# Dealing VectorE's and ScalarE's work anew beside one head's second product in a graph attention kernel

## The chip, the cores and the metric

The kernel runs on one core of a Trainium2 chip. The metric is the device time of one execution in microseconds (us), the median of several runs. The profile comes from one further execution, taken by the hardware profiler. TensorE (PE) multiplies matrices, VectorE (DVE) and ScalarE (ACT) work elementwise, GpSimd (POOL) issues here almost only DMAs that add to what they find (accumulating DMAs), and SyncE (SP) issues plain and transposing DMAs.

## The reference

Two graph attention layers over 512 nodes of 768 features, with a residual and a layer norm. The first layer has 8 heads, whose outputs are concatenated (512 x 6144) and pass through an ELU; the second has one head. All in float32.

```python
def gat_layer(x, W, a_s, a_d, b, edge_index, concat):
    n = x.shape[0]
    H, C = a_s.shape
    h = (x @ W).reshape(n, H, C)
    src, dst = (edge_index[0], edge_index[1])
    alpha_s = jnp.einsum('nhc,hc->nh', h, a_s)
    alpha_d = jnp.einsum('nhc,hc->nh', h, a_d)
    e = jax.nn.leaky_relu(alpha_s[src] + alpha_d[dst], NEG_SLOPE)
    m = jax.ops.segment_max(e, dst, num_segments=n)
    e = jnp.exp(e - m[dst])
    denom = jax.ops.segment_sum(e, dst, num_segments=n)
    alpha = e / (denom[dst] + EPS)
    msg = h[src] * alpha[:, :, None]
    out = jax.ops.segment_sum(msg, dst, num_segments=n)
    ...
h = gat_layer(x, W1, a_src1, a_dst1, b1, edge_list, concat=True)
h = jax.nn.elu(h)
out = gat_layer(h, W2, a_src2, a_dst2, b2, edge_list, concat=True)
...
x = _layernorm(x + out, axis=-1)
```

## The kernel before

The edges are counted once into a dense 512 x 512 table, so that attention becomes dense: for each head a matrix of 512 x 512 scores, a softmax along its rows, and a product with the head's features. The matrix lies in four tiles of 128 rows (tile 0 to 3). The order of all engines is written out by hand; each engine runs its own instructions strictly in that order and waits for others through semaphores.

A head goes through four stages. The first product makes its features (x times its 768 columns of W1). The scores of its attention are made beside other products. The aggregation multiplies features and attention and passes through the ELU to gT. The second product multiplies gT by the head's 768 rows of W2 and adds to h2, the input of the second layer. The first product and the second product run in a fast scheme with fewer multiplications: the operands are cut into thirds and sums of them are multiplied, 15 products named P0 to P14, in the order P13, P2, P8, P4, P12, P9, P6, P0, P1, P14, P10, P5, P11, P7, P3. This document numbers them 0 to 14 by that order and also speaks of them by name. Each has eight matmul instructions in the profile (L480).

The loop `for h in range(H - 1)` holds at h = 6 (`last`) the second product of the seventh head, with the scores of the eighth head beside it. For each product n of the loop, `multiply()` issues the matmuls, then the list `plan[n]` is issued, and `empty()` takes the result out of its PSUM bank into h2. The pieces:

- `empty()` is, by default, an addition on VectorE straight from PSUM (L493). For the pieces of h2 listed in `by_dma` it is a copy by ScalarE to a buffer in SBUF (L490) and an accumulating DMA from POOL (L491). In the seventh head only the piece (1, 2), which P13, P8 and P0 feed, goes by DMA; in the heads before also (0, 0), which P2 and P7 feed, and (0, 2). The 15 products belong to five chains, each with one PSUM bank: P13, P4, P6, P14, P7 share one, P2, P12, P0, P10, P11, P3 another, P1 and P5 a third, P8 and P9 have one each. A product can start when its chain's bank has been emptied.
- `sum_up(...)` issues on VectorE the sums of gT that a product reads (L1073, L1076); `of_b(...)` those of the weights (L170), of which only P3's is left for this stage; P7's is an accumulating DMA of POOL (L133) behind product 1.
- `score(t)` makes tile t of the scores on ScalarE (`lift`, L636). `scored(t)` is `leak` on VectorE (L640), `rank` on VectorE (L645, count and row maximum) and the exponential on ScalarE (L649), which also gives the row sums `den`.
- `weigh(q, t)` makes one over the row sum on VectorE (L878 and L879, `rden`) and, unless `scale=False`, multiplies the tile by it on VectorE (L881).
- The weighted tiles must be transposed into PT. Tiles 0 and 1 go by DMA: `turn_out` copies the tile (L898, ScalarE), SP issues a transposing DMA (L900), and `turn_in` copies the result into PT (L903, ScalarE). With `rden` given, `turn_out` first scales the tile on ScalarE (L895). Tiles 2 and 3 are turned by TensorE: `turn` is four transposes (L887) and a copy into PT by ScalarE (L888).

In the seventh head before, `weigh` with scaling follows products 7, 9, 11 and 13 for tiles 0 to 3; `turn_in` of tiles 0 and 1 follows products 12 and 13; `turn` of tile 2 stands ahead of product 14, that of tile 3 inside it, before its last two matmuls.

Behind product 14 `last_sum()` has POOL issue one accumulating DMA into w2r for the second layer (L118, 576 KB); SP loads x again (L99). Then the last aggregation (`aggregate`, L921) multiplies all of PT and the eighth head's features in six steps of 128 columns; beside it VectorE forms the second layer's logits from h2 (L424), and the second layer's products follow (L409, L1414).

Of the kernel before, what the change touches and what calls it, by code (L numbers as in the profile page):

```python
# [13 lines left out]
AF = mybir.ActivationFunctionType  # L14
# [23 lines left out]
def gat_pass(  # L38
# [16 lines left out]
    nc = tc.nc  # L55
    P = 128
    N, D = x.shape
    H = a_src1.shape[0]
# [373 lines left out]
    def by_halves(hs, XA, B_):  # L432
# [4 lines left out]
        def pair(p, i, start, empty):  # L437
            def multiply():
                if start:
# [17 lines left out]
                 P1=("z", (0, 1), -1.0), P10=("y", (1, 1), -1.0), P5=("z", (1, 1), 1.0), P14=("x", (0, 1), -1.0),  # L457
                 P11=("y", (0, 1), 1.0), P7=("x", (0, 0), -1.0), P3=("y", (0, 2), -1.0))
# [44 lines left out]

    def second_by_thirds(h, A_, B_):
        return by_thirds(h2, A_, B_, ("P13", "P2", "P8", "P4", "P12", "P9", "P6", "P0", "P1", "P14", "P10", "P5", "P11", "P7", "P3"),
                         False, ((1, 2), (0, 0), (0, 2)) if h + 2 < H else ((1, 2),))

    def second(A_, B_):

# [168 lines left out]
    if not general:  # L678
# [95 lines left out]
        for n, batch in enumerate(batches):  # L774
# [10 lines left out]
            while n < len(wants) and pos < wants[n]:  # L785
# [3 lines left out]
                multiply, empty, on_vector = items[pos]  # L789
# [17 lines left out]
            if n + 1 == len(batches):  # L807
                spread(0)
                q = [lift(0, t) for t in range(NT)]
# [11 lines left out]
    else:  # L821
# [26 lines left out]
        q = [lift(0, t) for t in range(NT)]  # L848
# [20 lines left out]
    def weigh(q, t, scale=True):  # L869

        if folded:
            den = dens.pop(t)
        else:
            den = small.tile([P, 1], F32, name="den")
            nc.vector.scalar_tensor_tensor(q, q, 1.0, cnt[:, t, :], op0=ALU.mult, op1=ALU.mult,
                                           accum_out=den)
        rden = small.tile([P, 1], F32, name="rden")
        nc.vector.tensor_scalar(rden, den, EPS_DEN, None, op0=ALU.add)  # L878
        nc.vector.reciprocal(rden, rden)  # L879
        if scale:  # L880
            nc.vector.tensor_scalar(q, q, rden, None, op0=ALU.mult)  # L881
        return rden

    def turn(q, t):
        ps = tr.tile([P, 512], F32, name="tr")
        for s in range(NT):
            nc.tensor.transpose(ps[:, s * P:(s + 1) * P], q[:, s * P:(s + 1) * P], ident)  # L887
        nc.scalar.copy(PT[:, :, t * P:(t + 1) * P], ps[:, :N].rearrange("p (s d) -> p s d", d=P))  # L888
# [4 lines left out]
    def turn_out(q, t, rden=None):  # L893
        if rden is not None:
            nc.scalar.activation(q, q, AF.Copy, scale=rden)  # L895
        apart = pS[:, t].rearrange("p k n -> p (k n)") if t < 3 else work.tile([P, N], F32, name="nr")
        apart = apart.bitcast(U16)
        nc.scalar.copy(apart.rearrange("p (h n) -> p h n", h=2), q.bitcast(U16).rearrange("p (n h) -> p h n", h=2))  # L898
        parted[t] = work.tile([P, N], F32, name="zr", bufs=3).bitcast(U16)
        nc.sync.dma_start(parted[t].rearrange("p (j d) -> p j d", d=P), apart, transpose=True)  # L900

    def turn_in(t):
        nc.scalar.copy(PT.rearrange("p s n -> p (s n)").bitcast(U16).rearrange("p (s n h) -> p s n h", s=NT, h=2)[  # L903
            :, :, t * P:(t + 1) * P, :], parted.pop(t).rearrange("p (h s d) -> p s d h", h=2, s=NT))
# [206 lines left out]
    def out_by_dma(t):  # L1111
        turn_out(q[t], t, weigh(q[t], t, scale=False))

    for h in range(H - 1):
        last = h + 2 == H
        q = {}
# [12 lines left out]
        if h == 0:  # L1129
            GA, gsums = left(gT, gS)  # L1130
            finish = mixed(0, AA, BB, [[besides[:1], [besides[1], sources[0]]], [[sources[1]], [sources[2]] + row],
                                       [besides[2:], list(targets)]])
            load_w1(2)()
            load_a(2, a_src1[2], a_dst1[2])
            attend = attended(0)
            pairs = by_halves(h2, GA, B2)
            for m, _ in pairs[:2]:
                m()
            pairs[0][1]()
            for f in finish:  # L1140
                f()
            gsums[0]()
            pairs[1][1]()
            gsums[1]()
            pending[0]()
            pairs[2][0]()
            gsums[2]()
            pairs[3][0]()
            gsums[3]()
            pending[1]()  # L1150
            pairs[2][1]()
            pairs[3][1]()
            fold_count(0)
            score(0)
            for n in range(2, 7):
                (m0, e0), (m1, e1) = pairs[2 * n:2 * n + 2]
                m0()
                m1()
                if n < 6:
                    scored(n - 2)  # L1160
                if n < 5:
                    score(n - 1)
                if n == 6:
                    turn_in(0)
                    out_by_dma(2)
                e0()
                if 3 < n < 6:
                    out_by_dma(n - 4)
                if n == 6:
                    out_by_dma(3)  # L1170
                    B2, sums2, load_pairs, load_first, load_rest = load_second(1)
                    load_pairs()
                    load_first()
                    load_rest()
                e1()
                if n < 5:
                    fold_count(n - 1)
        else:
            G, gsums = g_thirds(h)

            def of_b(*names):
                return [sums2.pop(p) for p in names if p in sums2]

            amid = [[], of_b("P6", "P2"), behind] if h == 1 else [of_b("P1"), [], of_b("P4")]
            finish = mixed(h, AA, BB, [[[sources[0]], [sources[1]] + amid[0]], [row, [targets[0]] + amid[1]], [amid[2], [targets[1]]]],
                           [gsums[p] for p in ("P13", "P8")])
            behind = []
            if not last:
                load_a(h + 2, a_src1[h + 2], a_dst1[h + 2])
                attend = attended(h)  # L1190
            pairs = second_by_thirds(h, G, B2)

            def sum_up(*names):
                return [gsums[p] for p in names]

            def at(f, *args):
                return [lambda: f(*args)]

            plan = {0: of_b("P6") + sum_up("P14") + finish[:1], 1: finish[1:] + of_b("P4") + sum_up("P12"), 2: sum_up("P9", "P7"),
                    3: sum_up("P1") + at(score, 0), 4: sum_up("P6"), 5: at(scored, 0) + at(score, 1), 6: of_b("P1") + sum_up("P10"),  # L1200
                    7: at(scored, 1) + at(score, 2), 8: sum_up("P5") + of_b("P3"), 9: at(scored, 2) + at(score, 3),
                    10: sum_up("P11"), 11: at(scored, 3), 12: [], 13: sum_up("P3")}
            if h > 1:
                plan[0][1:1] = [plan[13].pop()]
            behind_it = {1: of_b("P7")}

            def also(n, *what):
                plan[n] = plan.get(n, []) + list(what)

            for n, f in zip((8, 10), in_second):  # L1210
                also(n, f)
            if not last:
                for f in attend:
                    also(13, f)
            for n, (multiply, empty) in enumerate(pairs):
                if last and n == 14:
                    turn(q[2], 2)
                    multiply(lambda: turn(q[3], 3))
                else:
                    multiply()  # L1220
                for f in plan.get(n, []):
                    f()
                if last and n in (7, 9, 11):
                    weigh(q[(n - 7) // 2], (n - 7) // 2)
                    if n < 11:
                        turn_out(q[(n - 7) // 2], (n - 7) // 2)
                if last and n > 11:
                    if n < 14:
                        turn_in(n - 12)
                    if n == 13:  # L1230
                        weigh(q[3], 3)
                empty()
                if not last and n == 13:
                    turn_in(0)
                for f in behind_it.get(n, []):
                    f()
                if last:
                    continue
                if n in (7, 9, 11, 14):
                    out_by_dma(min(n - 7, 6) // 2)  # L1240
                if n == 5:
                    B2, sums2, load_pairs, load_first, load_rest = load_second(h + 1)
                    load_pairs()
                if n == 14:
                    rest_of_thirds()
                    reload_x()
                    load_first()
                    load_rest()
# [68 lines left out]
    finish = []  # L1317
# [150 lines left out]
```

## Time and profile before

| | |
|---|---|
| median of 3 runs | 639.59 us (639.29 to 639.63) |
| the profiled execution | 639.91 us, of which the span from the first to the last instruction is 638.0 us |
| second product of the seventh head, first product to the last aggregation's start | 526.22 to 556.53 us |
| last aggregation (L921) | 556.53 us to 579.09 us |
| mean granted TensorE clock | 0.995 |

The span is the time from the first instruction's start to the last one's end; times in the text are counted from its start. A timeline row gives an instruction's start, its duration, engine, line, operation, output and inputs and how many were merged; in square brackets stands the engine's idle time ahead of it and what ended that. Ends of matmuls are modelled by the profiler. Weight loads (PEld) run beside matmuls.

### The profile page before, as it was taken

Reading aid. Unit: us, or ns where it says so; the run is one execution under the profiler, and the core shown is the slowest. Engines: PE = TensorE matmul, PEld = TensorE weight load, DVE = VectorE, ACT = ScalarE, POOL = GpSimd, SP = SyncE. Lnnn points to the kernel's source line nnn. Section 1 sums busy time; section 2 is a strip of 40 time slices with the busy share of each in tenths; the row PEclk is TensorE's granted clock in tenths of the full one; section 3 lists DMA queues with packets and bytes.
Section 4 is the critical chain, followed back from the end, with each engine's and each line's share of the span. In section 5 each row is a group of like instructions: output and inputs, shape, how many; then the busy total and the mean of one; then the engine's idle time right before and its main releaser. Section 6 shows DMA issues by size and latency. Waiting matters only on the chain.

```text
span 638.0 us, 8411 instructions
## 1 busy us (share of the span) xinstructions
PE 623.7 (98%) x2725; PEld 477.2 (75%) x2725; DVE 523.3 (82%) x1112; ACT 329.8 (52%) x579; POOL 146.2 (23%) x174
## 2 busy tenths in 40 slices
PE   8999999999999999999999999999999999899995
PEld 5555586556888888888888888888888888645553
DVE  8979989788898878968896879878897879656775
ACT  4875775640658146741757055832756164443440
POOL 1300011023342332313352332413432302100000
PEclk9999999999999999999999999999999999999999
DMA  8993397789999998999899998999899983810122
GB/s 294 328 239 91 69 257 256 175 221 254 251 214 166 297 261 201 183 294 234 200 209 228 265 247 209 166 330 240 174 206 263 238 260 50 160 52 1 33 58 78
DMA packets 108207, 126.82 MB, mean 199 GB/s; under 512 B 41542, under 2 KB 89342, under 8 KB 107390
## 3 DMA queue, kind: packets, MB, share of 16 engines
q1 hardware_dynamic: 74718, 90.17, 45.3%
q0 software_dynamic: 33008, 35.46, 36.2%
q10 hardware_dynamic: 432, 0.59, 0.3%
q8 instruction: 23, 0.38, 0.2%
q14 instruction: 26, 0.21, 0.1%
HBM read 98.66 MB, written 2.90 MB: 159 GB/s over the span
## 4 chain that ended last, share of the span: by engine, by line
PE 87%; DVE 6%; DMA 3%; ACT 2%; issue 1%; SPq 0%; DVEq 0%; ACTq 0%
PE mm L480 40%; PE mm L974 18%; PE mm L409 16%; PE mm L921 4%; PE mm L1414 3%; PE held L409 2%; PE tr L742 1%; DMA zr<-pS 1%; DMA w2r<-in_L_gnn_W_dram 1%; DMA w2t<-in_L_gnn_a_dst_dram 1%; DVE h L493 1%; DVE q L645 1%; DVE q L640 1%; PE bc L276 1%; PE held L608 1%
## 5 line engine op out<-in xcount | busy, mean ns | idle before, releaser
L486 ACT ACTIVATE hs<-mm 128x512 f32<-128x512 f32 x30 | 17.9, 596 | 88.9 <-PE mm L480 70.8
L974 PE MATMUL mm<-PT,hs 128*128 128x256 f32 x252 | 61.3, 379 | 0.0
L649 ACT ACTIVATE q<-q,nmax 128x512 f32<-128x512 f32 x32 | 23.1, 722 | 60.2 <-DVE nmax L645 60.2
L493 DVE TENSOR_TENSOR hs<-hs,mm 128x512 f32<-128x512 f32 x45 | 30.8, 684 | 27.7 <-PE mm L480 26.1
L974 PEld LDWEIGHTS mm<-PT,hs 128*128 128x128 f32 x252 | 47.8, 190 | 7.2 <-ACT u L978 0.3
L491 POOL DMA_DIRECT2D h<-pass x22 | 26.5, 1313 | 89.2 <-ACT pass L490 79.3
L493 DVE TENSOR_TENSOR h<-h,mm 128x512 f32<-128x512 f32 x57 | 38.9, 684 | 7.3 <-PE mm L480 6.8
L974 PE MATMUL mm<-pS,gS 128*128 128x256 f32 x168 | 43.1, 379 | 0.0
L903 ACT COPY PT<-zr 128x1024 uint16<-128x1024 uint16 x34 | 39.2, 1154 | 5.8 <-DMA zr<-pS 5.2
L480 PE MATMUL mm<-w2r,gT 128*128 128x256 f32 x160 | 37.9, 385 | 0.0
L480 PE MATMUL mm<-w2r,xT 128*128 128x256 f32 x160 | 37.8, 379 | 0.0
L133 POOL DMA_DIRECT2D w1t<-in_L_gnn_W_dram x18 | 29.4, 1651 | 29.6 <-PE mm L409 26.8
L974 PEld LDWEIGHTS mm<-pS,gS 128*128 128x128 f32 x168 | 31.9, 190 | 4.3
L480 PE MATMUL mm<-w1t,hs 128*128 128x256 f32 x144 | 34.3, 381 | 0.5 <-DVE h L493 0.5
L480 PEld LDWEIGHTS mm<-w2r,gT 128*128 128x128 f32 x160 | 29.6, 190 | 6.6 <-DVE hs L493 3.0
L480 PE MATMUL mm<-w1r,hs 128*128 128x256 f32 x144 | 34.2, 379 | 0.0
L480 PE MATMUL mm<-w1r,gS 128*128 128x256 f32 x144 | 34.0, 379 | 0.0
L480 PEld LDWEIGHTS mm<-w2r,xT 128*128 128x128 f32 x160 | 30.4, 190 | 4.1
L978 ACT COPY u<-mm 128x256 f32<-128x256 f32 x21 | 7.8, 371 | 45.7 <-PE mm L974 45.7
L480 PEld LDWEIGHTS mm<-w1t,hs 128*128 128x128 f32 x144 | 27.1, 190 | 5.1 <-DVE h L493 1.3
L716 DVE TENSOR_SCALAR os<-nodes,idx 128x512 bf16<-128x512 f16 x104 | 29.1, 352 | 1.4 <-PE tr L742 1.4
L480 PEld LDWEIGHTS mm<-w1r,gS 128*128 128x128 f32 x144 | 27.4, 190 | 3.7
(281 smaller groups left out, 1543.4 us busy)
## 6 DMA issues: line engine op xcount, KB each, us to landing
w2r<-in_L_gnn_W_dram SPq DMA_DIRECT2D x48, 384.0 KB
w1r<-in_L_gnn_W_dram SPq DMA_DIRECT2D x43, 384.0 KB
gT<-xd SPq DMA_DIRECT2D x5, 1280.0 KB
w1t<-in_L_gnn_W_dram SPq DMA_DIRECT2D x24, 256.0 KB
h<-pass POOLq DMA_DIRECT2D x22, 256.0 KB, 3.9
w1t<-in_L_gnn_W_dram POOLq DMA_DIRECT2D x18, 256.0 KB, 5.8
w2t<-in_L_gnn_W_dram SPq DMA_DIRECT2D x15, 256.0 KB
w2t<-in_L_gnn_W_dram POOLq DMA_DIRECT2D x15, 256.0 KB, 9.1
```

Source lines behind the costliest of these rows:

```text
L133: nc.gpsimd.dma_start(o, i, accum_op=ALU.add)
L409: nc.tensor.matmul(ps[:, :HALF], A_[p][:, k, i * P:(i + 1) * P], B_[p][:, k, :], start=start and k == 0, stop=k == HK - 1, skip_group_chec ...
L480: nc.tensor.matmul(bank[chain][:, i * TH:(i + 1) * TH], A_[p][:, k, i * P:(i + 1) * P], B_[p][:, k, :], start=first and i == k == 0, stop= ...
L486: nc.scalar.activation(out(o), ps, AF.Copy, scale=sign)
L491: nc.gpsimd.dma_start(out(o), part, accum_op=ALU.add)
L493: nc.vector.tensor_tensor(out(o), out(o), ps, op=ALU.add if sign > 0 else ALU.subtract)
L649: nc.scalar.activation(q, q, AF.Exp, bias=nmax, scale=-1.0, accum_out=dens[t])
L716: nc.vector.tensor_scalar(o, nodes, idx[:, c:c + 1], None, op0=ALU.is_equal)
L903: nc.scalar.copy(PT.rearrange("p s n -> p (s n)").bitcast(U16).rearrange("p (s n h) -> p s n h", s=NT, h=2)[:, :, t * P:(t + 1) * P, :], p ...
L921: nc.tensor.matmul(ps[:, :N], HS[h][:, s, c * P:(c + 1) * P], PT[:, s, :], start=(s == 0), stop=(s == NT - 1))
L974: nc.tensor.matmul(bank[p][:, :HN], A_[p][:, k, c * P:(c + 1) * P], B_[p][:, k, :], start=over is None and k == 0, stop=k == 1, skip_group ...
L1414: nc.tensor.matmul(ps[:, :cols.stop - cols.start], PT[:, s, t * P:(t + 1) * P], h2[:, s, cols], start=(s == 2), stop=(s == 1))
```

## The change

In the seventh head's second product alone:

- The piece (0, 0) of h2, fed by P2 and P7, is emptied by a ScalarE copy and an accumulating DMA instead of VectorE.
- The plan is written anew for this head: the sums of P14 and P3 go from product 0 to products 5 and 11, the other sums, too, partly change places, the scores start behind product 1 instead of 3, tile by tile one to two products earlier, and P3's weight sum goes from product 8 to 12.
- All four tiles are scaled by ScalarE: tiles 0 and 1 in `turn_out` behind products 7 and 9, tiles 2 and 3 by a new helper `scale` behind products 11 and 12.
- Tile 2 is turned ahead of product 13 and tile 3 ahead of product 14. Both `turn_in` follow product 13, behind tile 2's turn and ahead of tile 3's in ScalarE's order.
- As POOL works in order, its DMA for P7 now stands ahead of L118 of `last_sum()`.

```diff
     def second_by_thirds(h, A_, B_):
         return by_thirds(h2, A_, B_, ("P13", "P2", "P8", "P4", "P12", "P9", "P6", "P0", "P1", "P14", "P10", "P5", "P11", "P7", "P3"),
-                         False, ((1, 2), (0, 0), (0, 2)) if h + 2 < H else ((1, 2),))
+                         False, ((1, 2), (0, 0), (0, 2)) if h + 2 < H else ((1, 2), (0, 0)))
...
+    def scale(t):
+        nc.scalar.activation(q[t], q[t], AF.Copy, scale=weigh(q[t], t, scale=False))
+
...
+            third_sum = of_b("P3")
             plan = {0: of_b("P6") + sum_up("P14") + finish[:1], 1: finish[1:] + of_b("P4") + sum_up("P12"), 2: sum_up("P9", "P7"),
                     3: sum_up("P1") + at(score, 0), 4: sum_up("P6"), 5: at(scored, 0) + at(score, 1), 6: of_b("P1") + sum_up("P10"),
-                    7: at(scored, 1) + at(score, 2), 8: sum_up("P5") + of_b("P3"), 9: at(scored, 2) + at(score, 3),
+                    7: at(scored, 1) + at(score, 2), 8: sum_up("P5") + third_sum, 9: at(scored, 2) + at(score, 3),
                     10: sum_up("P11"), 11: at(scored, 3), 12: [], 13: sum_up("P3")}
             if h > 1:
                 plan[0][1:1] = [plan[13].pop()]
+            if last:
+                plan = {0: finish[:1], 1: finish[1:] + sum_up("P12") + at(score, 0), 2: sum_up("P9", "P7"), 3: sum_up("P1"),
+                        4: sum_up("P6") + at(scored, 0) + at(score, 1), 5: sum_up("P14"), 6: sum_up("P10") + at(scored, 1) + at(score, 2),
+                        7: at(out_by_dma, 0) + sum_up("P5"), 8: sum_up("P11") + at(scored, 2) + at(score, 3), 9: at(out_by_dma, 1),
+                        10: at(scored, 3), 11: at(scale, 2) + sum_up("P3"), 12: third_sum + at(scale, 3), 13: at(turn_in, 0) + at(turn_in, 1)}
...
             for n, (multiply, empty) in enumerate(pairs):
-                if last and n == 14:
-                    turn(q[2], 2)
-                    multiply(lambda: turn(q[3], 3))
-                else:
-                    multiply()
+                if last and n > 12:
+                    turn(q[n - 11], n - 11)
+                multiply()
                 for f in plan.get(n, []):
                     f()
-                if last and n in (7, 9, 11):
-                    weigh(q[(n - 7) // 2], (n - 7) // 2)
-                    if n < 11:
-                        turn_out(q[(n - 7) // 2], (n - 7) // 2)
-                if last and n > 11:
-                    if n < 14:
-                        turn_in(n - 12)
-                    if n == 13:
-                        weigh(q[3], 3)
                 empty()
```

## The prediction

> **What bounds the kernel now.** I read the page first: one core, TensorE busy nearly throughout, so a change beside it can only win back time in which TensorE stands still or runs slowly.
>
> ```profile
> span 638.0 us, 8411 instructions
> PE 623.7 (98%) x2725; PEld 477.2 (75%) x2725; DVE 523.3 (82%) x1112; ACT 329.8 (52%) x579; POOL 146.2 (23%) x174
> ```
>
> Then the timeline of TensorE around the seventh head's second product. Its fifteen products start at 526.22. The last two matmuls of product 14 start at 553.11, and the last aggregation (L921) starts after an idle 2.83 us, the largest hole between matmuls in the run.
>
> ```profile
> 553.11 0.60 PE L480 MATMUL mm<-w1r,hs 128*128 128x256 f32 x2
> 556.53 22.56 PE L921 MATMUL mm<-PT,hs 128*128 128x512 f32 x48 [2.83 <-ACT PT L888]
> ```
>
> The chain of waits says what the aggregation waited for: tile 1's copy for the turning DMA (L898), that DMA, which took 7.34 us, ScalarE's copy-in (L903), and both copies of the TensorE-turned tiles 2 and 3 (L888), queued behind it.
>
> ```profile
> 546.02 0.94 ACT pS L898
> 546.97 0.02 issue
> 546.98 7.34 DMA zr<-pS
> 554.33 0.02 issue
> 554.35 1.16 ACT PT L903
> 555.51 0.98 ACT PT L888 x2
> 556.49 0.04 issue
> 556.53 22.56 PE mm L921 x48
> ```
>
> Why 7.34 us? The DMA view, over the 3.52 us after that issue and over tile 0's issue, one fence each: in the first stretch no packet of SP's queue q1 moves, and POOL's q0 has 96.1% of the engines.
>
> ```profile
> q0 software_dynamic: 363, 0.52, 96.1%
> ```
>
> ```profile
> q1 hardware_dynamic: 1056, 0.26, 42.4%
> ```
>
> The second line is tile 0's transfer: all its 1056 packets lie within 543.06 to 545.80, 2.74 us from the issue. q0 in the first stretch is L118, the 576 KB accumulation into w2r that POOL issued at 544.53, ahead of tile 1's transfer.
>
> Last, the windows of the granted clock (columns: stretch, length, busy time and instructions of PE, PEld, DVE, ACT, POOL, clock, DMA share, GB/s).
>
> ```profile
> 549.90:553.31 3.41, 3.41 (x21) 3.02 (x20) 2.04 (x6) 0.66 (x1) 0.00 (x0) 1.00 1.39 135
> 553.31:556.72 3.41, 0.58 (x3) 0.19 (x2) 0.76 (x2) 2.13 (x3) 0.00 (x0) 1.00 0.56 162
> 556.72:560.13 3.41, 3.41 (x5) 1.35 (x5) 0.00 (x0) 0.00 (x0) 0.00 (x0) 0.50 1.00 392
> 560.13:563.54 3.41, 3.41 (x10) 1.50 (x9) 0.00 (x0) 1.58 (x3) 0.00 (x0) 1.00 0.07 29
> 628.40:631.81 3.41, 2.56 (x16) 2.18 (x14) 2.78 (x8) 0.00 (x0) 0.00 (x0) 1.00 0.31 120
> ```
>
> After a stretch with TensorE busy for 0.58 of 3.41 us, the next 3.41 us run at clock 0.50: five matmuls where the next stretch has ten. The hole costs twice: 2.83 us empty, and a slow start. From the aggregation's start to the next product (578.93) are 22.40 us; its 48 matmuls at the 0.429 us pitch of the later ones would take 20.59. The slow start is 1.81 us. All that can be had here is 2.83 + 1.81, and small stalls in front of products 10 and 12 (0.45 us: product 13 starts 22.99 us after product 0, where 1.83 and twelve times 1.726 make 22.54): some 5 us.
>
> **The change, part by part.** Prices are start to start, from rows of this stretch and of the sixth head's, which already scales on ScalarE.
>
> VectorE loses the emptying of P2 and P7 (L493, 0.60 each) and four scalings (L881, 0.40, 0.60, 0.40, 0.40): 3.0 us. ScalarE gains two copies (L490, 0.49 each), two scalings in front of the DMA copy (L895 then L898 of the same tile, 0.74) and two in front of a turn (0.62 by the same row): 3.7 us. ScalarE is busy for 9.86 of the 19 us from 538 to 557, so there is room; where it is not free is the order, below.
>
> POOL gets two more accumulations (P2's and P7's, L491, 256 KB). P2's stands ahead of B's P7 sum (L133, 531.30 before), which moves back by about 1 us; that sum took 4.5 us and product 13 reads it at 549. P8's accumulation waits for P13's landing (534.2) as before. P7's stands ahead of L118: L118 moves from 544.53 to about 554, behind the copy of P7. Its reader is the last layer's P7 product, at 594.64 now and 589.8 then; the longest landing of that line is 17.1 us, so it is in by 571. Cost nothing.
>
> Now the order, replayed with the rows' prices. TensorE unstalled: 526.22, a first product of 1.83, fourteen at 1.726, two turns of 0.44: product 13 ends at 551.1, the turn of tile 3 at 551.4, product 14 at 553.25.
>
> VectorE: the sums of P14 and P3 no longer precede the finish, so L915 starts at 528.6 instead of 529.8. Then P12, P9, P7, P1 to 532.9; P4's emptying waits for product 3 (533.4). Leak 0 at 534.6 (535.76 before): tile 0's q was made at 530.2, behind P13's copy on ScalarE. That q needs the row broadcast, whose issue at 523.38 lies seven us earlier. From there each tile costs VectorE leak, rank, rden (0.72, 0.62, 0.27) and about three L493 or sums (0.60 each); leaks fall at 534.6, 538.4, 541.8 and 544.8, the last held for 0.2 us by tile 3's q on ScalarE. Rank 3 ends at 546.2. Then P10's emptying, rden 2 (547.1), P3's sum, P5's emptying, B's P3 sum, rden 3 (549.2), P11's emptying (549.8).
>
> ScalarE: scale 0 at 541.2, behind tile 2's q; copy 0 ends 542.9. Then P0's copy (ends 543.45; product 10 reads that bank at 543.5, a margin of nothing and a stall of at most 0.1, as before), exp 2, q 3, scale 1 at 544.7, copy 1 ends 546.46; exp 3 at 546.4, scale 2 at 547.1, and scale 3, which waits for rden 3, at 549.2 to 549.9. Behind scale 3 the queue holds L888 of tile 2 (549.8), L903 twice (550.3, 551.4), P7's copy (552.45) and L888 of tile 3 (552.9 to 553.5): with scale 3 six instructions, 4.3 us, all in front of the aggregation. P10's emptying ends 546.84; product 12 follows in that bank at 547.05. The turn of tile 2 needs scale 2 (547.9) at 548.8, that of tile 3 scale 3 (549.9) at 550.95: both in time.
>
> Turning DMAs: tile 0 issued 543.0, tile 1 546.5. L118 is gone from that stretch; what is left is P0's 256 KB accumulation, which before was issued 0.8 us after tile 0's and let it pass in 2.74 us. Bounds for tile 1: 2.74 (tile 0's row) and 7.34 us; I take 2.74, as the thing that stood in the way has gone: landed 549.2, wanted at 551.4.
>
> So the aggregation starts at the later of TensorE's 553.25 and ScalarE's 553.5 plus 0.06: 553.56 instead of 556.53, **2.97 us** earlier. TensorE is idle for 0.3 us, less than the 0.85 us not busy in the last window shown, which was followed by clock 1.00; so the slow start goes too, **1.81 us**. Sum 4.8 us. After that everything hangs on TensorE: the DVE view shows holes of 0.9, 0.6 and 2.0 us before 581, and nothing else moves.
>
> The halved clock also has a page in the Trainium skill: TensorE: Matmul & The Clock Gate, section "What's actually happening", gives at least one idle window of about 3.4 us as what halves the clock. The hole here is 2.83 us and TensorE worked for 0.58 us of the window, and yet the next one ran at 0.50: read strictly, the rule would leave the clock alone, and a change that only closes the hole would give 2.97 us; the trace speaks against it.
>
> The profiled run took 639.91 us (span 638.0 and 1.9 around it), 0.32 over the median of 639.59. 639.91 - 4.8 = 635.1, in terms of the median **634.8 us**.
>
> **The rivals.** (a) The scores don't come that fast. Between leaks the seventh head has 3.46, 3.92 and 4.11 us now, the sixth 3.40, 3.45 and 3.52, my replay 3.7, 3.4, 3.0. At 3.45 for the last, everything behind moves by 0.4 us (635.2). At 4.11 throughout, leak 3 falls at 547.0, 2.1 late; the hole is 2.4 us and the clock may halve again: 636.9 to 638.7. For: VectorE and ScalarE wait for one another four times. Against: the sixth head's rows, with the same scaling. Chance 0.11.
>
> (b) The slow start isn't the hole's doing. Then only 2.97 us come: 636.6. Against: the halved stretch follows the one nearly idle window before the end, and no other. By the Trainium skill's rule above this would be the outcome. Chance 0.04.
>
> (c) Tile 1's transfer is late for another reason, 7.34 us as now. It lands at 553.8; L903, P7's copy and L888 put the start at 556.0, the hole and the clock stay: 639.1, no change to speak of. Chance 0.04.
>
> (d) Slower: P7's accumulation. It is issued at 553.05, as SP starts the five loads of 384 KB that wait for product 14. The first logits of the last layer (L424) read those columns at 559.65, and VectorE stands in order behind them. L491's landings go from 3.6 to 10.4 us in this trace, the long ones beside such loads: 556.7 to 563.5. VectorE's holes before 581 take up 3.4 us, so up to a landing at 563 it is free, and at 10.4 us it costs 0.5. It eats the whole gain at 567.9 (559.65 + 3.4 + 4.8), 14.8 us after the issue, and past that the kernel is slower: at 17.1 us, the longest landing of a 576 KB accumulation, the last layer starts 7.1 us late and the time is 641.9. Chance 0.03; with what I don't see, slower gets 0.05.
>
> **How the numbers follow.** My forecast has 0.78: 634.8, and for itself 634.2 (start at TensorE's 553.25, nothing late on ScalarE) to 635.9. The range reaches into (a) and over (b): 634.0 to 637.0; left out are the late part of (a), (c) and (d). This kernel's three runs lie within 0.34 us, so about 0.2%, 1.3 us, can be told from no change. Faster by more than that (below 638.3): the forecast, (a) nearly whole, (b): 0.91. Same 0.04, slower 0.05.
>
> **What would show it.** In the profile after: no idle over 0.5 us in front of L921, and released by L888; the aggregation's 48 matmuls in 20.8 instead of 22.56 us, clock 1.00 there; tile 1's DMA off the chain; L118 issued after 553; ScalarE without a hole from scale 3 to L888. Wrong would be: a DMA still on the chain in front of L903, a hole on ScalarE in front of scale 3 with rden 3 after 550, or L424 waiting for the accumulation into h.

## The result and the profile after

The changed kernel takes 634.93 us (median of 6 runs, 634.20 to 635.21) against 639.61 us: a ratio of 0.993, 95% interval 0.9912 to 0.9947. The forecast was 634.8 us. The profiled execution took 634.52 us with a span of 632.7 us.

TensorE's timeline, the two rows that answer to those of before (start, duration, what, in brackets the idle time ahead and what ended it):

```profile
550.80 1.89 PE L480 MATMUL mm<-w1r,hs 128*128 128x256 f32 x8
552.97 20.87 PE L921 MATMUL mm<-PT,hs 128*128 128x512 f32 x48 [0.28 <-ACT PT L888]
```

The hole of 2.83 us is 0.28 us, and the aggregation's 48 matmuls take 20.87 instead of 22.56 us. The first product starts at 525.56 here, at 526.22 before: what lies ahead of the change differs from execution to execution (525.15 to 526.24 in the ten profiles of this case), so stretches are compared, not places. The whole of that difference is there before the first L409 matmul, which starts at 10.24 to 11.37 us; from it to product 0 all ten take 514.85 to 514.94 us. From product 0 to the aggregation's start it is 27.41 us (30.31 before, -2.90), from there to the next product 20.71 us (22.40, -1.69), and from there to the end 59.0 us in both. The two differences make 4.6 us.

The chain of waits in front of the aggregation no longer has a DMA in it:

```profile
548.38 0.17 DVE rden L879
...
548.64 0.72 ACT q L1115
549.36 0.47 ACT PT L888
549.83 0.33 ACT PT L903
550.16 0.63 issue
550.79 1.16 ACT PT L903
551.96 0.49 ACT pass L490
552.45 0.48 ACT PT L888
```

It is ScalarE's queue from tile 3's scaling on, without idle time (the 0.63 us of "issue" lie inside the first of two L903, which ScalarE's timeline shows as busy throughout).

The DMA view of the 3.52 us after the issue of tile 1's turning DMA (queue, packets, MB, share of 16 engines), the same stretch that before showed q0 alone:

```profile
q1 hardware_dynamic: 1053, 0.26, 36.4%
q0 software_dynamic: 101, 0.09, 16.5%
```

1053 of the transfer's 1056 packets are through; before, none was. And the windows of the clock around the start (stretch, length, busy times, then clock, DMA share, GB/s):

```profile
549.56:552.97 3.41, 3.13 (x17) 2.42 (x15) 0.24 (x1) 3.36 (x5) 0.22 (x1) 1.00 0.00 0
552.97:556.38 3.41, 3.41 (x8) 1.63 (x9) 0.52 (x2) 0.00 (x0) 2.27 (x2) 1.00 0.74 186
```

The clock stays at 1.00.

One thing about the time before must be known to read it. The 42 runs of the kernel before that stood beside the experiments fall into two groups: 15 had a mean clock of 0.997 or more and a median of 637.33 us (637.09 to 638.45), the other 27 had 0.991 to 0.996 and times from 638.78 us on, and the 19 of them at 0.995 or 0.996 a median of 639.82 us. The profiled execution, with its halved clock behind the hole, is one of the second group (0.995). So about two executions in three seem to be slowed behind the hole, and the median is of such a one. No execution of the first group was profiled. Nor is the hole's slow start all that parts the groups: they lie 2.5 us apart, and it costs 1.7 to 1.8. Part of the rest may be the start of an execution, where the profiles differ by up to 1.1 us; this was not tested. Against the first group the change is worth 637.33 - 634.93 = 2.4 us. The changed kernel's twelve times lie within 1.1 us.

### The profile page after: what moved, and what is told of

Same layout as the page of the kernel before. It is cut to its first block, busy times and chain, and to the rows that moved or that the text cites. A ratio compares the mean times of both kernels' runs of the same rounds, so it can differ in the third digit from the quotient of the medians.

```text
span 632.7 us, 8415 instructions
## 1 busy us (share of the span) xinstructions
PE 621.1 (98%) x2725; PEld 476.6 (75%) x2725; DVE 520.1 (82%) x1106; ACT 333.1 (53%) x585; POOL 148.6 (23%) x176
## 4 chain that ended last, share of the span: by engine, by line
PE 85%; DVE 7%; DMA 4%; ACT 2%; issue 1%; SPq 1%; DVEq 0%; POOLq 0%; ACTq 0%
PE mm L480 39%; PE mm L974 17%; PE mm L409 17%; PE mm L921 3%; PE mm L1412 3%; DMA w2r<-in_L_gnn_W_dram 3%; PE held L409 2%; PE tr L742 1%; DMA w2t<-in_L_gnn_a_dst_dram 1%; DVE h L493 1%; DVE q L640 1%; DVE q L645 1%; DVE hs L1073 1%; PE bc L276 1%; PE held L608 1%
## 5 line engine op out<-in xcount | busy, mean ns | idle before, releaser
L493 DVE TENSOR_TENSOR h<-h,mm 128x512 f32<-128x512 f32 x55 | 37.6, 684 | 9.6 <-PE mm L480 9.0
L903 ACT COPY PT<-zr 128x1024 uint16<-128x1024 uint16 x34 | 39.1, 1155 | 2.4 <-DMA zr<-pS 1.8
```

What stands on the lines that cost most here:

```text
L493: nc.vector.tensor_tensor(out(o), out(o), ps, op=ALU.add if sign > 0 else ALU.subtract)
```

## The experiments

Two theories were set against each other. Theory L: the place of one DMA, L118, in POOL's queue decides, as it kept tile 1's turning DMA waiting. Rival O: the new order of VectorE and ScalarE brings the aggregation forward, and L118 is incidental. e1 to e4 stood beside runs of before with a median of 639.48 us, e5 to e7 and the changed kernel's second set beside 639.57; each ratio is to the runs of before that stood beside it. The table has, from each profile, the stretch from product 0 to the aggregation's start, the hole in front of it, tile 1's turning DMA from issue to landing, and the stretch from the aggregation to the next product.

| kernel | product 0 to L921, us | hole | tile 1's DMA | L921 to next | time, us | ratio to before (95%) |
|---|---|---|---|---|---|---|
| before | 30.31 | 2.83 | 7.34 | 22.40 | 639.48 | |
| the changed one | 27.41 | 0.28 | 4.23 | 20.71 | 634.93 | 0.9930 (0.9912 to 0.9947) |
| e1: piece (0, 0) by DMA only | 28.41 | 1.11 | 4.95 | 20.70 | 635.19 | 0.9943 (0.9923 to 0.9962) |
| e2: new order only | 29.42 | 2.29 | 7.38 | 22.40 | 638.63 | 0.9993 (0.9977 to 1.001) |
| e3: changed, L118 forward | 29.54 | 2.41 | 7.01 | 22.40 | 638.77 | 0.9992 (0.9974 to 1.001) |
| e4: before, L118 early | 27.54 | 0.24 | 4.53 | 20.71 | 634.97 | 0.9942 (0.9920 to 0.9964) |
| e5: before, hole filled | 30.27 | 0.20 | 7.29 | 20.71 | 637.94 | 0.9981 (0.9966 to 0.9996) |
| e6: scaling on VectorE | 27.74 | none | 2.78 | 20.71 | 634.55 | 0.9927 (0.9905 to 0.9950) |
| e7: copy-in sooner | 26.99 | none | 4.46 | 20.70 | 634.77 | 0.9926 (0.9903 to 0.9949) |
| the changed one again | 27.42 | 0.29 | 4.46 | 20.70 | 634.29 | 0.9928 (0.9905 to 0.9952) |

**e1, one line of the change alone.** The kernel before, with P2 and P7 emptied through ScalarE and POOL:

```diff
-                         False, ((1, 2), (0, 0), (0, 2)) if h + 2 < H else ((1, 2),))
+                         False, ((1, 2), (0, 0), (0, 2)) if h + 2 < H else ((1, 2), (0, 0)))
```

> The kernel before with one line of the change: the piece (0, 0) of h2, fed by P2 and P7, is emptied by ScalarE and an accumulating DMA, so that POOL has P7's DMA ahead of the 576 KB accumulation (L118), which then issues at about 552 instead of 544.5. Theory L (the place of L118 in POOL's queue decides, by keeping tile 1's turning DMA waiting): that DMA takes under 4.5 us instead of 7.3, the last aggregation starts at about 553.8 of the old count instead of 556.5, the clock is not halved behind it: 639.6 - 2.7 - 1.7 = 635.2 us. Rival O (the new order of VectorE and ScalarE brings the aggregation forward, L118 is incidental): only the 0.6 us of P2's emptying are gained, 638.5 to 639.6 us.

635.19 us, as theory L had it; rival O falls. ScalarE's timeline shows what the old order still costs: it waits for the DMA, and both L888 come behind P7's copy.

```profile
550.89 1.16 ACT L903 COPY PT<-zr 128x1024 uint16<-128x1024 uint16 x1 [1.58 <-DMA zr<-pS]
551.96 0.59 ACT L490 ACTIVATE pass<-mm 128x512 f32<-128x512 f32 x1
552.45 1.06 ACT L888 COPY PT<-tr 128x512 f32<-128x512 f32 x2
```

**e2, the rest of the change without that line.**

```diff
-                         False, ((1, 2), (0, 0), (0, 2)) if h + 2 < H else ((1, 2), (0, 0)))
+                         False, ((1, 2), (0, 0), (0, 2)) if h + 2 < H else ((1, 2),))
```

> The changed kernel without that one line: P2 and P7 emptied by VectorE as before, all of the new order kept. L118 issues again at about 544, between tile 0's and tile 1's turning DMAs. Theory L: tile 1's DMA takes about 7.3 us again, the aggregation starts some 2 us later than in the changed kernel, with the clock halved behind the hole 3.7 us: 637 to 638.7 us. Rival O: within 0.7 us of the changed kernel, 634.9 to 635.6 us.

638.63 us; the interval of the ratio includes 1. POOL issued L118 at 544.49 and tile 1's DMA, issued at 546.51, landed 7.38 us later. The new order alone is worth 0.9 us in the stretch (30.31 to 29.42). The medians can't tell this; within the group at a clock of 0.995 or 0.996, e2's eight runs have a median of 638.70 us against the 639.82 of before.

**e3, the whole change with L118 put back ahead of P7's DMA.** It alters nothing but POOL's order:

```diff
                 empty()
+                if last and n == 8:
+                    last_sum()
...
         else:
-            last_sum()
             B2, sums2 = right(W2[H - 1], "w1")
```

> The changed kernel in full, but L118 is issued behind product 8, so that it stands in POOL's queue ahead of P7's DMA and starts at about 544. Nothing moves on VectorE, ScalarE and TensorE. Theory L: tile 1's turning DMA is 7 us again instead of 4.2, ScalarE's L903 waits for it, then come P7's copy and L888; the aggregation starts 2.3 us later and the clock is halved or not: 637.2 to 639.1 us. Rival O: as the changed kernel, 634.9 us.

638.77 us: 3.8 us of the change's gain are gone again. The DMA view of the 3.52 us after tile 1's issue has q0 and no packet of q1, as before the change, and ScalarE and TensorE wait:

```profile
q0 software_dynamic: 371, 0.50, 93.5%
```

```profile
553.30 1.16 ACT L903 COPY PT<-zr 128x1024 uint16<-128x1024 uint16 x1 [2.02 <-DMA zr<-pS]
```

```profile
555.49 2.36 PE L921 MATMUL mm<-PT,hs 128*128 128x512 f32 x3 [2.41 <-ACT PT L888]
```

**e4, the kernel before with L118 issued behind product 2**, and nothing else moved:

```diff
+                if last and n == 2:
+                    last_sum()
                 empty()
...
         else:
-            last_sum()
             B2, sums2 = right(W2[H - 1], "w1")
```

> The kernel before with L118 issued behind product 2 instead of behind the loop, and nothing else: it issues at about 532 and has landed by 541, ahead of both turning DMAs. Theory L: tile 1's DMA takes 2.7 to 4.3 us, the aggregation is released by tile 3's turn at about 553.9 instead of 556.5, clock 1.00 behind it: 635.3 us, nearly all of the change's gain from moving one DMA. Rival O: no gain, 639.6 us.

634.97 us, the change's time to 0.1 us, from moving one DMA (issued at 531.0, landed 538.8) to a place where nobody waits for what it delays: P8's accumulation into h2 landed 6.4 us after its issue instead of 3.6.

```profile
550.56 1.16 ACT L903 COPY PT<-zr 128x1024 uint16<-128x1024 uint16 x1 [1.16 <-DMA zr<-pS]
551.62 1.11 ACT L888 COPY PT<-tr 128x512 f32<-128x512 f32 x2
```

```profile
552.78 4.56 PE L921 MATMUL mm<-PT,hs 128*128 128x512 f32 x10 [0.24 <-ACT PT L888]
```

**e5, the hole filled.** The kernel before, with three matmuls (six instructions in the profile) that nobody reads behind product 14:

```diff
         else:
+            idle_ = bc.tile([P, 512], F32, name="bc")
+            for _ in range(3):
+                nc.tensor.matmul(idle_, ident, xT[:, 0, :], start=True, stop=True)
             last_sum()
```

> The kernel before with three more float32 matmuls of 128x512 behind product 14, into an unused PSUM bank and read by nobody: TensorE works for about 2.6 of the 2.83 us in which it waits for the last aggregation, which starts when it did. If the hole is what halves the clock, the aggregation's 48 matmuls take 20.7 instead of 22.4 us: 637.9 us. If the slow start has another cause: 639.6 us.

637.94 us. The aggregation starts when it did (30.27 us after product 0), released late by the same DMA, but runs at full speed. TensorE's rows and the windows of the clock:

```profile
553.22 2.74 PE L1308 MATMUL bc<-xT,ident 128*128 128x512 f32 x6
556.16 1.12 PE L921 MATMUL mm<-PT,hs 128*128 128x512 f32 x2 [0.20 <-ACT PT L888]
```

```profile
552.98:556.39 3.41, 3.21 (x9) 1.37 (x8) 0.76 (x2) 2.13 (x3) 0.00 (x0) 1.00 0.60 207
556.39:559.80 3.41, 3.41 (x9) 1.50 (x9) 0.00 (x0) 0.00 (x0) 0.00 (x0) 1.00 0.89 301
```

None of e5's twelve times lies above 638.68 us. So the hole is what halves the clock, and its two prices come apart: the slow start is 22.40 - 20.71 = 1.69 us in the profiles and 639.57 - 637.94 = 1.6 in the medians; the hole itself, with the small stalls ahead of it, is 30.27 - 27.42 = 2.85 us in the profiles, and 3.0 or 3.65 in the medians, by the first or the second set of the changed kernel.

**e6, the scaling back on VectorE**, the rest of the change kept:

```diff
+    def out_scaled(t):
+        weigh(q[t], t)
+        turn_out(q[t], t)
+
     def scale(t):
-        nc.scalar.activation(q[t], q[t], AF.Copy, scale=weigh(q[t], t, scale=False))
+        weigh(q[t], t)
...
-                        7: at(out_by_dma, 0) + sum_up("P5"), ...
+                        7: at(out_scaled, 0) + sum_up("P5"), ...
-                        ... 9: at(out_by_dma, 1),
+                        ... 9: at(out_scaled, 1),
```

> The changed kernel with the four scalings back on VectorE (L881, 0.40 to 0.60 us each), the order kept. Theory L: tile 3 is scaled about 1.5 us later on VectorE, at about 550.2, while its turn is wanted at 550.4; ScalarE's queue in front of the aggregation gets shorter: at most 0.5 us slower than the changed kernel, 634.9 to 635.4 us. Rival S (the scaling by ScalarE is what lets the scores come sooner): 1.8 us slower, 636.7 us, more with the clock.

634.55 us, 0.26 us from the changed kernel beside it (634.29), which these times can't tell from nothing; the stretch is 0.32 us longer, as TensorE stands still for 0.56 us ahead of a product instead of 0.29 ahead of the aggregation. Who scales the tiles is worth no more than that here; rival S falls.

**e7, tile 0's copy-in between the scalings of tiles 2 and 3.**

```diff
-                        ... 11: at(scale, 2) + sum_up("P3"), ...
+                        ... 11: at(scale, 2) + at(turn_in, 0) + sum_up("P3"), ...
-                        ... 13: at(turn_in, 0) + at(turn_in, 1)}
+                        ... 13: at(turn_in, 1)}
```

> The changed kernel with tile 0's copy into PT (L903) issued by ScalarE between the scalings of tiles 2 and 3, where it waits 1.39 us for VectorE, instead of behind tile 2's turn. If ScalarE's six instructions behind that wait set the aggregation's start, as the replay has it, it starts 0.28 us sooner, with no hole left: 634.6 us. If not, no change: 634.9 us.

In the profile the hole is gone and the stretch is 26.99 us, 0.43 shorter than in the changed kernel beside it, so ScalarE's six instructions did set the start. In the times it can't be seen: 634.77 us against 634.29, ranges 633.84 to 634.81 and 634.13 to 635.20. ScalarE's rows, the second now in the wait that was there:

```profile
547.20 0.72 ACT L1115 ACTIVATE q<-q,rden 128x512 f32<-128x512 f32 x1
547.83 1.15 ACT L903 COPY PT<-zr 128x1024 uint16<-128x1024 uint16 x1
549.31 0.72 ACT L1115 ACTIVATE q<-q,rden 128x512 f32<-128x512 f32 x1 [0.34 <-DVE rden L879]
```

**The changed kernel again**, for e5 to e7 to be compared with:

> The changed kernel once more, on the chip of the three others, to compare them with: 634.9 us.

634.29 us (634.13 to 635.20), 0.64 below the six earlier runs: differences of half a microsecond between kernels are not to be read from these medians.

## Why the prediction was right, step by step

- What held the aggregation. Named as tile 1's DMA behind L118, from one row of the DMA view; e3 and e4 show it, each by moving L118 alone, in opposite directions.
- The replay of the order. Counted from product 0, leaks were put at 8.4, 12.2, 15.6 and 18.6 us and came at 8.5, 12.2, 15.6 and 18.65; rden 3 was put at 23.0 and came at 22.98; the aggregation at 27.34, and came at 27.41. ScalarE's tail was the later of the two limits, as forecast, and e7 shows it.
- The earlier start: 2.97 us forecast, 2.90 measured. Of these 2.55 are the hole (2.83 to 0.28), the other 0.35 small stalls of TensorE ahead of it (from product 0 to the hole 27.48 us before, 27.13 after). The slow start: 1.81 forecast, 1.69 measured in the profiles, and 1.6 us in e5's medians. Rival (b) is refuted by e5.
- Tile 1's DMA: I took 2.74 us and it took 4.23 to 4.46. A term mis-sized, without effect as it was wanted 4.9 us after its issue; ScalarE came to it at 550.79 and it had landed at 550.12. In e1 and e4, where ScalarE is there sooner, L903 waits 1.58 and 1.16 us for it.
- Rival (d): P7's accumulation landed 8.3 us after its issue, and VectorE waited 1.93 us for it in front of the logits, inside the 3.4 us that were reckoned as free. The later stretches are unmoved.

```profile
561.15 0.96 DVE L424 SCALAR_TENSOR_TENSOR scr<-h,w2t 128x768 bf16<-128x768 f32 x1 [1.93 <-DMA h<-pass]
```

- What I had not seen is how little of the change was needed. The working gave VectorE's 3.0 us and ScalarE's 3.7 a long account, and they are worth at most 1.0 us in the stretch (e1 against the changed kernel) and 0.13 where L118 is put early (e4). And the 1.81 us were taken as if every execution paid them, where about two in three seem to.
- Luck, and a wrong reading. The three runs that gave a noise of 0.2% (639.29 to 639.63) and the profiled one all came out of the second group; the 42 later runs go from 637.09 to 641.55 us. So the noise was read too small: single runs span 4.5 us, and a median of three can fall into either group. The gain of 4.7 us in the medians is that over an execution of the second group. The forecast of the time after, 634.8 us, does not hang on it: it takes the slow start off an execution that had it. The chances that were given add up to 1.02.

## What to carry to other kernels

When the chain shows a DMA that takes several times what its like takes elsewhere in the trace, look at what the other queues move in that time before dealing any engine's work anew: here one call moved by twelve products gave the whole gain. A hole in TensorE is to be priced with the matmuls behind it. A time that falls into two groups is a reason to look for such a hole. An accumulating DMA added in front of a reader is free only as far as the reader's engine has holes; count these.

## What the runs showed of the hardware

A transposing DMA on SP's queue moved no packet in the 3.5 us behind its issue while POOL's queue, with the accumulating DMA of 576 KB issued 2.0 to 2.5 us ahead of it, had 94 to 96% of the engines (before and e3; in the first 0.6 to 1.0 us also the end of P0's accumulation). Its first packet came 3.7 us after the issue in before and 4.2 us in e3, instead of 1.2 us in the changed kernel: the two transfers hardly shared the engines, they took turns. Why, no run here shows.

A hole of 2.3 to 2.8 us in TensorE halved the clock for the next 3.4 us in the profiles of before, e2 and e3. In the stretch of 3.41 us ahead of the halved one TensorE was busy for 0.58 us in before, 1.00 in e3 and 1.12 in e2. With 2.30 us busy (e1, whose hole is 1.11 us) or 2.56 us (before, near its end) the clock stayed at 1.00. Two stretches of e2 and two of e1:

```profile
553.23:556.64 3.41, 1.12 (x4) 0.55 (x4) 0.76 (x2) 1.64 (x2) 0.00 (x0) 1.00 0.65 206
556.64:560.05 3.41, 3.41 (x6) 1.35 (x5) 0.00 (x0) 0.00 (x0) 0.00 (x0) 0.50 0.96 352
```

```profile
550.39:553.80 3.41, 2.30 (x13) 1.72 (x12) 0.76 (x2) 2.62 (x4) 0.96 (x2) 1.00 0.08 14
553.80:557.21 3.41, 3.41 (x9) 1.50 (x9) 0.00 (x0) 0.00 (x0) 1.54 (x2) 1.00 0.91 247
```

Not every execution was slowed. By their granted clocks and times together, 27 of 42 were in before, 8 of 12 in e3 (638.71 us and more, the others up to 637.26) and 9 of 12 in e2 (637.98 and more, the others up to 637.26). The mean clock alone does not tell it: the last 1.9 to 4.8 us of every profile run at 0.50 too, behind the last matmul, and e5's profile has a mean of 0.996 with no other halved stretch. The Trainium skill, TensorE: Matmul & The Clock Gate, section "What's actually happening", says that the window in which TensorE's activity is watched runs freely and does not start with the kernel; the two groups of times agree with that. Its idle window of about 3.4 us as the condition does not agree with the traces: 2.29 us of idle time (e2) were enough.

In nine of the ten profiles an instruction-load packet of 16 KB (queue q8) fell into tile 1's transfer. Where L118 was out of the way (the changed kernel twice, e1, e4, e7) the transfer then took 4.2 to 5.0 us; in e6, where it came after the transfer, 2.78 us. In the changed kernel 1024 of the 1056 packets had started within 2.3 us of the issue, as all of tile 0's had; the last 32 followed up to 3.6 us, behind a packet of q8 that started at 1.75 us and took 1.02. That the packet is the cause was not tested. The view of e6 over the 2.78 us has no line of q8:

```profile
q1 hardware_dynamic: 1056, 0.26, 41.8%
q0 software_dynamic: 20, 0.00, 1.8%
```
